# Experts' tokens loaded as squares of 32x32 and turned on VectorE, in a fused GNN, attention and mixture-of-experts kernel

## The chip, the cores and the metric

The kernel runs on one core of a Trainium2 chip. The metric is the device time of one execution in microseconds. A core has five engines with an instruction stream each: TensorE (PE, its weight loads are shown as PEld), VectorE (DVE), ScalarE (ACT), GpSimd (POOL) and SyncE (SP), which here only issues transfers. The transfers themselves run on 16 DMA engines.

## The reference, cut to what matters

One layer on 4096 tokens of 256 floats, all in fp32: an aggregation over a 4096x4096 adjacency matrix, causal attention with four heads, and then the part that the change touches, a mixture of 8 experts of which every token uses two.

```python
flat = _rmsnorm(x, ln2_w).reshape(-1, Cx)
probs = jax.nn.softmax(flat @ router_w.T, axis=-1)
tp, ti = jax.lax.top_k(probs, TOPK)
tp = tp / (jnp.sum(tp, axis=-1, keepdims=True) + 1e-09)
weights = jnp.sum(tp[..., None] * jax.nn.one_hot(ti, NE, dtype=flat.dtype), axis=1)
out = jnp.zeros_like(flat)
for e in range(NE):
    hh = jax.nn.silu(flat @ w1[e].T) * (flat @ w3[e].T)
    out = out + weights[:, e:e + 1] * (hh @ w2[e].T)
return x + out.reshape(Bx, Tx, Cx)
```

The hidden width is 682. The kernel computes an expert only for the tokens that chose it.

## The kernel before

Three stages follow each other: the aggregation to about 510 us, attention over eight blocks of 512 tokens to about 1027 us, the experts to the end. The stages overlap at their edges: the last attention block's normalization and output product run as "steps" between the products of the first expert groups.

**Lists.** As tokens are finished in attention they are written to a table `lists` in DRAM, sorted by expert. A row has 265 floats (`ROW` = 256 + 1 + 8): the token, its row number, and its 8 gates.

**Groups.** The experts' work is cut into groups of rows of one expert: 256 rows for the first 25 (`NW`), 128 for the rest; 42 are run (`NM`). `TURNS` is the order: nine large ones, then large and small mixed, mostly in turn (a "pair" below; at three places two small ones follow one large, a "double pair"), three large ones last. Loops run over k, a place in that order. `SEVEN` are the large groups from k = 4 to 39, whose second product is made of seven half-size products (Strassen's manner); `SPLIT13`, 13 of them (k from 12 to 39), do the same in the first product. Its sums of weights are made by GpSimd (`sums13`, L1463 to L1466), its sums of inputs by VectorE (`sums_x`, L1480).

**What a group needs.** `load13` (L1382, 1.4 MB) and `load2` (L1388, 0.77 MB) bring an expert's weights, `load_rows` (L1399) the group's rows, one transfer with a row on each partition. The expert and the first row come from a table, through registers. All three are issued by SP, each into one of five buffers in turn.

**Preparing a group.** `prepare(k)` turns the tokens so that features lie on partitions: TensorE transposes (L1413) into a PSUM tile `tx`, then ScalarE scales by the norm's weights into `xT` (L1419), `sums_x` where the group is in `SPLIT13`, and VectorE picks the expert's gate (`pick`, L1427, and a reduction, L1432). `hidden(k)` (L1698, L1704, L1705) or `hidden_seven(k)` (products L1525, ScalarE's copies of banks L1531, adds L1534, silu, multiplications L1563 and L1564) makes the first product and the gating, and calls `prepare` for the next group: after the first block of products where the next PSUM bank is free early (`early`, and before `SEVEN`), and otherwise at its end; `hidden_seven` does so after its third products. `combine(k-1)` (L1754, or L1655 with VectorE's adds L1663 to L1669) makes the second product, ScalarE or VectorE multiplies by the gate (L1765, L1771), and GpSimd adds the rows to DRAM at the row numbers (scatter, L1776).

**The loop.** Turn k: `hidden(k)` with `prepare(k+1)`, `combine(k-1)`, then GpSimd writes `sent` (L1910) and SP copies it to `sent_dram` (L1911), which makes SP wait until GpSimd has issued the scatters, then SP issues `load2(k+4)`, `load13(k+5)`, `load_rows(k+4)`; then GpSimd's `sums13`. Every engine executes in the order of its own queue. A framework puts in the semaphores; each DMA takes one of eight in rotation and waits for the one that had it before.

**The start of the experts.** `begin_experts` (L1789) issues the first loads late in attention (at 1018 us of the trace). `prepare(0)` is put two places before attention's end. The steps at the hand-over are: VectorE's totals of exponentials (L810), then for the last block the adding of two parts (L833), a reciprocal of the denominators (L845), a multiplication (L846), and then TensorE's output product po (L901).

Two lines tell much of the queues:

```python
nc.gpsimd.memset(sent, 0.0)
nc.sync.dma_start(sent_dram, sent)
```

Of the kernel before, what the change touches and what calls it, by code (L numbers as in the profile page):

```python
# [17 lines left out]
P = 128  # L18
N = 4096
C = 256  # L20
# [46 lines left out]
def fast_kernel(  # L67
# [618 lines left out]
    with (  # L686
# [14 lines left out]
        pt_all = sp.tile([P, 9 * 1024], F32, name="pt_all")  # L701
        late = sp.tile([P, 2 * (NF + 1) * GR + 4 * GR + 5 * 2 * ROW], F32, name="late")
        LATE_XT, LATE_ROWS = 2 * (NF + 1) * GR, 2 * (NF + 1) * GR + 4 * GR
        ring = [pt_all[:, n * 1024 : (n + 1) * 1024] for n in range(9)]
# [345 lines left out]
        def join(inst, group):  # L1050
            tc.add_to_no_dep_group(group, inst.ins)
# [320 lines left out]
        w2s = [a.rearrange("p (k c) -> p k c", k=NF + 1) for a in at2]  # L1372
        rows, hidden_of, inputs_of, expert_of, gates_of = {}, {}, {}, {}, {}

# [11 lines left out]
        def load2(k):  # L1386
# [4 lines left out]
            )  # L1391

        def load_rows(k):
            i = TURNS[k]
            n = halves(i)
            at = entry(table[0:1, 0, i : i + 1], NE * REG - (GR if i < NW else 0))
            r = late[:, LATE_ROWS + k % 5 * 2 * ROW : LATE_ROWS + (k % 5 + 1) * 2 * ROW]
            r = r.rearrange("p (h c) -> p h c", h=HALF)
            get = nc.sync.dma_start(  # L1399
                r[:, 0:n, :], lists[bass.ds(at, n * P), :].rearrange("(h p) c -> p h c", p=P)  # L1400
            )
            if i < NA:
                free(get, "late writes", "the rows of the first groups are whole by then")
                join(get, "first reads")
            rows[i] = r

        def prepare(k, pool=p_y, tag="y"):
            i = TURNS[k]
            n = halves(i)
            tr = pool.tile([P, 2, n, P], F32, tag=tag, name=f"tx_{i}")  # L1410
            for h in range(n):
                for c in range(2):
                    nc.tensor.transpose(  # L1413
                        tr[:, c, h, :], rows[i][:, h, c * P : (c + 1) * P], ident
                    )
# [11 lines left out]
            nc.vector.tensor_mul(  # L1427
                pick, rows[i][:, 0:n, C + 1 : ROW],
                mine[:, i : i + 1, :].to_broadcast([P, n, NE]),
            )  # L1430
            gates_of[i] = ex.tile([P, n, 1], F32, tag="gt", name=f"gt_{i}", bufs=3)
            nc.vector.tensor_reduce(gates_of[i], pick, AX.X, ALU.add)  # L1432
# [35 lines left out]

        def sums_x(k, tr):

# [6 lines left out]
            for dst, c, h, less in (  # L1477
                ("T1", 0, 1, "B11"), ("T2", 1, 1, "T1"), ("T3", 1, 1, "B12"), ("T4", 1, 0, "T2"),
            ):
                nc.vector.scalar_tensor_tensor(  # L1480
                    m[dst], tr[:, c, h, :], ln2_sb[:, c : c + 1], m[less],
                    op0=ALU.mult, op1=ALU.subtract,
# [3 lines left out]
        def hidden_seven(k, step, behind):  # L1486
# [99 lines left out]
            if behind is not None:  # L1586
                prepare(behind, p_ms, "ms")
            gated(two)
# [83 lines left out]
        def hidden(k, step=None, behind=None):  # L1672
# [3 lines left out]
            hT = hTs[k % 2][:, :, 0:n]  # L1676
            free_bank = k >= SEVEN[0]
            early = n == P and not (k - 1 in SEVEN and k - 2 in SEVEN)

            for q in range(0, NF + 1, 2):  # L1680
# [38 lines left out]
            )  # L1719
            if behind is not None and free_bank and not early:  # L1720
                prepare(behind, p_ms, "ms")
            hidden_of[i] = hT
# [3 lines left out]
        def combine(k):  # L1726
# [34 lines left out]
            for h in range(n):  # L1761
# [12 lines left out]
                at = bass.IndirectOffsetOnAxis(ap=r[:, h, C : C + 1].bitcast(I32), axis=0)  # L1774
                nc.gpsimd.memset(gap, 0.0)  # L1775
# [64 lines left out]
        for b in ORDER[:-1]:  # L1840
# [9 lines left out]
        later.setdefault(PLACES - 2, []).append(  # L1850
            lambda: [prepare(0, p_ms, "ms")] + [nc.gpsimd.memset(t[:, NF, :], 0.0) for t in hTs]
        )
# [36 lines left out]
        for k in range(NM):  # L1889
# [775 lines left out]
```

## Time and profile before

| | |
|---|---|
| time, median of three runs | 1532.2 us (1532.18 to 1532.7) |
| the profiled execution | 1532.31 us |
| its span in the trace | 1530.5 us |
| experts' stage | from about 1027 us to the end |
| a pair in that stage | 21.5 us |
| transposes of tokens on TensorE | 134 |

A profile is of one execution, and the span is the time from its first to its last instruction; 1.8 us lie around it. Times in the trace count from the span's start. A line of the timeline has start and length in us, the engine, the source line, the operation, what it writes and reads, shapes, and in brackets how long the engine stood idle before it and which instruction released it. Matmuls overlap each other in TensorE, so the length of one record (273 ns for a transpose) is more than what it costs in a row of them. The last 20 us hold scatters to the output that wait for a copy of the sums from DRAM to DRAM, issued at 1492.04 us in turn order (L1923).

### The profile page before, as it was taken

Reading aid. Unit: us, or ns where it says so; the run is one execution under the profiler, and the core shown is the slowest. Engines: PE = TensorE matmul, PEld = TensorE weight load, DVE = VectorE, ACT = ScalarE, POOL = GpSimd, SP = SyncE. Lnnn points to the kernel's source line nnn. Section 1 sums busy time; section 2 is a strip of 40 time slices with the busy share of each in tenths; the row PEclk is TensorE's granted clock in tenths of the full one; section 3 lists DMA queues with packets and bytes.
Section 4 is the critical chain, followed back from the end, with each engine's and each line's share of the span. In section 5 each row is a group of like instructions: output and inputs, shape, how many; then the busy total and the mean of one; then the engine's idle time right before and its main releaser. Section 6 shows DMA issues by size and latency. Waiting matters only on the chain. (4 is left out here: it accounts for less than half of the span.)

```text
span 1530.5 us, 28132 instructions
## 1 busy us (share of the span) xinstructions
PE 1518.1 (99%) x10925; PEld 1122.9 (73%) x10925; DVE 1056.4 (69%) x2182; ACT 555.6 (36%) x989; POOL 556.8 (36%) x641
## 2 busy tenths in 40 slices
PE   9999999999999999999999999999999999999997
PEld 8888888888888544444444444358899999999996
DVE  7764665755755677779879878785565777677762
ACT  2102012021021455655665655653122433343341
POOL 2102022121221331374554553442424445545342
PEclk9999999999999999999999999999999999999999
DMA  6334444543544000010011011048777787787845
GB/s 240 131 130 151 160 141 148 161 153 127 179 141 151 5 1 23 22 58 30 30 58 37 28 38 36 23 166 297 220 204 219 225 275 254 225 274 248 271 129 134
DMA packets 69595, 212.16 MB, mean 139 GB/s; under 512 B 17898, under 2 KB 45930, under 8 KB 55818
## 3 DMA queue, kind: packets, MB, share of 16 engines
q1 hardware_dynamic: 55914, 191.99, 36.4%
q0 software_dynamic: 12720, 17.47, 6.5%
q8 instruction: 88, 1.44, 0.4%
q10 hardware_dynamic: 816, 0.79, 0.2%
q14 instruction: 57, 0.47, 0.1%
HBM read 184.48 MB, written 27.13 MB: 138 GB/s over the span
## 5 line engine op out<-in xcount | busy, mean ns | idle before, releaser
L782 PE MATMUL sc<-qT_all,kT 64*64 64x512 f32 (+3 forms) x2304 | 282.1, 557 | 0.5 <-ACT pt_all L790 0.3
L532 PE MATMUL acc<-a,g 128*128 128x256 f32 x1024 | 244.0, 379 | 0.0
L532 PEld LDWEIGHTS acc<-a,g 128*128 128x128 f32 x1024 | 193.5, 190 | 31.8 <-issue 6.7
L782 PEld LDWEIGHTS sc<-qT_all,kT 64*64 64x64 f32 x2304 | 91.2, 133 | 128.6 <-issue 109.2
L790 ACT ACTIVATE pt_all<-sc 128x1024 f32<-128x1024 f32 (+3 forms) x157 | 148.8, 955 | 96.7 <-PE sc L782 94.6
L1776 POOL DMA_INDIRECT acc_dram<-y,late x40 | 62.8, 1571 | 178.0 <-ACT y L1765 118.5
L532 PE MATMUL acc<-more_sums,g 128*128 128x256 f32 x512 | 126.3, 379 | 0.0
L810 DVE TENSOR_TENSOR late<-late,pt_all 128x1024 f32<-128x1024 f32 (+3 forms) x91 | 107.5, 1181 | 24.3 <-POOL pt_all L792 9.8
L433 ACT COPY qT_all<-tr 128x512 f32<-128x512 f32 x30 | 16.2, 588 | 259.1 <-PE tr L431 259.1
L532 PEld LDWEIGHTS acc<-more_sums,g 128*128 128x128 f32 x512 | 97.2, 190 | 13.2
L824 PE MATMUL y_first<-pt_all,vv 64*64 64x512 f32 (+3 forms) x448 | 106.6, 554 | 0.0
L625 POOL TENSOR_TENSOR rot<-rot,tables 128x512 f32<-128x512 f32 x21 | 33.9, 1615 | 198.6 <-ACT rot L621 158.4
L1698 PE MATMUL h<-late,qT_all 128*128 128x256 f32 (+1 forms) x616 | 105.2, 327 | 0.0
L824 PE MATMUL y_second<-pt_all,vv 64*64 64x512 f32 (+3 forms) x436 | 104.2, 555 | 0.0
L1698 PEld LDWEIGHTS h<-late,qT_all 128*128 128x128 f32 x616 | 94.0, 191 | 9.6 <-ACT late L1419 0.8
L1060 POOL DMA_INDIRECT lists<-row,slots x64 | 87.4, 1366 | 17.1 <-issue 14.3
L1705 DVE TENSOR_TENSOR late<-si,h 128x256 f32<-128x256 f32 (+2 forms) x87 | 40.0, 467 | 73.7 <-ACT si L1704 42.7
L1704 ACT ACTIVATE si<-h 128x256 f32<-128x256 f32 (+2 forms) x87 | 36.5, 421 | 145.1 <-PE h L1698 142.2
L824 PE MATMUL y_third<-pt_all,vv 64*64 64x512 f32 (+3 forms) x372 | 88.7, 555 | 0.0
L621 ACT ACTIVATE rot<-pq 32x512 f32<-32x512 f32 x84 | 49.5, 589 | 82.6 <-DVE qT_all L619 43.6
L810 DVE TENSOR_TENSOR sum_all<-sum_all,pt_all 128x1024 f32<-128x1024 f32 (+3 forms) x51 | 56.0, 1097 | 15.5 <-POOL pt_all L792 9.2
L790 ACT ACTIVATE late<-sc 128x1024 f32<-128x1024 f32 (+3 forms) x55 | 50.9, 927 | 41.4 <-PE sc L782 38.4
(490 smaller groups left out, 3350.7 us busy)
## 6 DMA issues: line engine op xcount, KB each, us to landing
a<-in_adj_dram SPq DMA_DIRECT2D x64, 1024.0 KB
qT_all<-in_w_dram SPq DMA_DIRECT2D x18, 1408.0 KB
pt_all<-in_w_dram SPq DMA_DIRECT2D x16, 1408.0 KB
res_all<-in_w_dram SPq DMA_DIRECT2D x17, 768.0 KB
pt_all<-in_w_dram SPq DMA_DIRECT2D x16, 768.0 KB
res_all<-in_w_dram SPq DMA_DIRECT2D x8, 1408.0 KB
qT_all<-in_w_dram SPq DMA_DIRECT2D x9, 768.0 KB
late<-lists SPq DMA_DIRECT2D x25, 265.0 KB
```

The source lines that it names most:

```text
L532: nc.tensor.matmul(acc[bank][:, at, :], g[jb][:, right, k, :], m[left][:, k, :], start=(jb == 0 and k == 0 and at == 0), stop=(jb == NB - ...
L621: nc.scalar.activation(rot[n * Q : (n + 1) * Q, :], pj[(n ^ 1) * Q : ((n ^ 1) + 1) * Q, :], AF.Copy, scale=1.0 if n % 2 else -1.0,)
L625: nc.gpsimd.tensor_mul(rot, rot, tables[b][:, 1, :])
L782: nc.tensor.matmul(ps[k * HP : (k + 1) * HP, j, :w], kT[sb][hd, i * P + k * HP : i * P + (k + 1) * HP], qT[b][hd, p, off:], start=True, st ...
L790: nc.scalar.activation(pt[:, :, :w], ps[:, :, :w], AF.Exp, scale=HD ** -0.5)
L810: nc.vector.tensor_add(sums[b, p][:, :, off:], before[:, :, off:], pt[:, :, : 512 - off])
L824: nc.tensor.matmul(accs[b, p][k][hd, off:], vv[sb][some, i, hd], pt[some, j, : 512 - off], start=(s == order_of(b)[0]), stop=(s == order_o ...
L1060: put = nc.gpsimd.indirect_dma_start(out=lists[:, :], out_offset=bass.IndirectOffsetOnAxis(ap=chosen[b][:, k, t, :], axis=0), in_=flats[b] ...
L1698: nc.tensor.matmul(ps[m % 2][:, m // 2 - q, :], w13_sb[:, c, m * P : (m + 1) * P], xT[:, c, :], start=(c == 0), stop=(c == 1),)
L1704: nc.scalar.activation(si[:, 0:both, :], ps[0][:, 0:both, :], AF.Silu)
L1705: nc.vector.tensor_mul(hT[:, q : q + both, :], si[:, 0:both, :], ps[1][:, 0:both, :])
L1776: put = nc.gpsimd.indirect_dma_start(out=(acc_dram if k < NM - LAST else out)[:, :], out_offset=at, in_=y[:, h, :], in_offset=None, comput ...
```

## The change

Tokens are no longer loaded as rows. `load_squares(k)` issues eight transfers for a group: for each quarter of the partitions (32 of them) and each half of the features. A partition of the first transfer holds, of one token of each 32, the 32 features of one square; each piece read from DRAM is 32 floats, 128 bytes. Then one VectorE transpose, which turns every 32x32 square in place, gives features on partitions. It writes into the room that the squares of group k+4 use later (five rooms in turn), and ScalarE and `sums_x` read it from SBUF instead of PSUM. `load_rows` loads only the 9 last floats of each row. In `prepare` nothing is left for TensorE, and no PSUM bank is needed, so the two conditions on the bank go and `prepare(k+1)` always stands after the first block of `hidden(k)`. The column of the row number in the scatter becomes 0. `begin_experts` has a new order, with the first narrow rows behind w13(1).

```diff
+        KEPT = ROW - C
+        LATE_XT = 2 * (NF + 1) * GR
+        LATE_Z = LATE_XT + 4 * GR
+        LATE_ROWS = LATE_Z + 5 * 2 * C
+        late = sp.tile([P, LATE_ROWS + 5 * 2 * KEPT], F32, name="late")
...
+        def squares_room(k):
+            return late[:, LATE_Z + k % 5 * 2 * C : LATE_Z + (k % 5 + 1) * 2 * C]
+
+        def load_squares(k):
+
+            i = TURNS[k]
+            n = halves(i)
+            at = rows_at[i] = entry(
+                table[0:1, 0, i : i + 1], NE * REG - (GR if i < NW else 0)
+            )
+            z = squares_room(k)[:, 0 : n * C].rearrange("p (c m d) -> p c m d", c=2, d=Q)
+            tokens = lists[bass.ds(at, n * P), 0:C].rearrange(
+                "(m i) (c g d) -> g c i m d", i=Q, c=2, d=Q
+            )
+            for g in range(4):
+                for c in range(2):
+                    loaded(
+                        i, nc.sync.dma_start(z[g * Q : (g + 1) * Q, c], tokens[g, c])
+                    )
...
-            get = nc.sync.dma_start(
-                r[:, 0:n, :], lists[bass.ds(at, n * P), :].rearrange("(h p) c -> p h c", p=P)
-            )
+            loaded(i, nc.sync.dma_start(
+                r[:, 0:n, :],
+                lists[bass.ds(rows_at.pop(i), n * P), C:].rearrange("(h p) c -> p h c", p=P),
+            ))
...
-        def prepare(k, pool=p_y, tag="y"):
+        def prepare(k):
             i = TURNS[k]
             n = halves(i)
-            tr = pool.tile([P, 2, n, P], F32, tag=tag, name=f"tx_{i}")
-            for h in range(n):
-                for c in range(2):
-                    nc.tensor.transpose(
-                        tr[:, c, h, :], rows[i][:, h, c * P : (c + 1) * P], ident
-                    )
+            turned = squares_room(k + 4)[:, 0 : n * C]
+            nc.vector.transpose(turned, squares_room(k)[:, 0 : n * C])
+            turned = turned.rearrange("p (c i) -> p c i", c=2)
             xT = late[:, LATE_XT + k % 2 * 2 * GR : LATE_XT + k % 2 * 2 * GR + 2 * n * P]
             xT = xT.rearrange("p (c i) -> p c i", c=2)
             for c in range(2):
                 nc.scalar.activation(
-                    xT[:, c, :], tr[:, c].rearrange("p h i -> p (h i)"), AF.Copy,
-                    scale=ln2_sb[:, c : c + 1],
+                    xT[:, c, :], turned[:, c, :], AF.Copy, scale=ln2_sb[:, c : c + 1]
                 )
             inputs_of[i] = xT
             if k in SPLIT13:
-                sums_x(k, tr)
+                sums_x(k, turned)
             pick = ex.tile([P, n, NE], F32, tag="pick", name=f"pick_{i}")
             nc.vector.tensor_mul(
-                pick, rows[i][:, 0:n, C + 1 : ROW],
+                pick, rows[i][:, 0:n, 1:KEPT],
                 mine[:, i : i + 1, :].to_broadcast([P, n, NE]),
             )
...
                 if q == 0 and behind is not None:
-                    if not free_bank:
-                        prepare(behind)
-                    elif early:
-                        prepare(behind, p_ms, "ms")
+                    prepare(behind)
...
-            if behind is not None and free_bank and not early:
-                prepare(behind, p_ms, "ms")
...
         def begin_experts():
             make_table(NB - 1, True, 0, NA)
-            load_rows(0)
+            load_squares(0)
             load13(0)
-            load_rows(1)
+            load_squares(1)
             load2(0)
             load13(1)
-            load_rows(2)
+            for k in range(2):
+                load_rows(k)
+            load_squares(2)
             load2(1)
-            load_rows(3)
+            load_squares(3)
+            for k in range(2, 4):
+                load_rows(k)
...
             if k + 4 < NM:
+                load_squares(k + 4)
                 load_rows(k + 4)
```

More of the change, by code (lines that the diff above doesn't have):

```diff
@@ L701, in fast_kernel @@
         pt_all = sp.tile([P, 9 * 1024], F32, name="pt_all")
-        late = sp.tile([P, 2 * (NF + 1) * GR + 4 * GR + 5 * 2 * ROW], F32, name="late")
-        LATE_XT, LATE_ROWS = 2 * (NF + 1) * GR, 2 * (NF + 1) * GR + 4 * GR
+        KEPT = ROW - C
[3 more added lines that the diff above has]
+        late = sp.tile([P, LATE_ROWS + 5 * 2 * KEPT], F32, name="late")
         ring = [pt_all[:, n * 1024 : (n + 1) * 1024] for n in range(9)]
@@ L1372, in fast_kernel @@
         w2s = [a.rearrange("p (k c) -> p k c", k=NF + 1) for a in at2]
-        rows, hidden_of, inputs_of, expert_of, gates_of = {}, {}, {}, {}, {}
+        rows, hidden_of, inputs_of, expert_of, gates_of, rows_at = {}, {}, {}, {}, {}, {}
         def halves(i):
@@ L1391, in load2, with loaded @@
             )
+        def loaded(i, get):
+            if i < NA:
+                free(get, "late writes", "the rows of the first groups are whole by then")
+                join(get, "first reads")
+        def squares_room(k):
[15 more added lines that the diff above has]
+                    )
         def load_rows(k):
@@ L1395, in load_rows @@
             n = halves(i)
-            at = entry(table[0:1, 0, i : i + 1], NE * REG - (GR if i < NW else 0))
-            r = late[:, LATE_ROWS + k % 5 * 2 * ROW : LATE_ROWS + (k % 5 + 1) * 2 * ROW]
+            r = late[:, LATE_ROWS + k % 5 * 2 * KEPT : LATE_ROWS + (k % 5 + 1) * 2 * KEPT]
             r = r.rearrange("p (h c) -> p h c", h=HALF)
-            get = nc.sync.dma_start(
-                r[:, 0:n, :], lists[bass.ds(at, n * P), :].rearrange("(h p) c -> p h c", p=P)
-            )
-            if i < NA:
-                free(get, "late writes", "the rows of the first groups are whole by then")
-                join(get, "first reads")
+            loaded(i, nc.sync.dma_start(
+                r[:, 0:n, :],
+                lists[bass.ds(rows_at.pop(i), n * P), C:].rearrange("(h p) c -> p h c", p=P),
+            ))
             rows[i] = r
-        def prepare(k, pool=p_y, tag="y"):
+        def prepare(k):
             i = TURNS[k]
             n = halves(i)
-            tr = pool.tile([P, 2, n, P], F32, tag=tag, name=f"tx_{i}")
-            for h in range(n):
-                for c in range(2):
-                    nc.tensor.transpose(
-                        tr[:, c, h, :], rows[i][:, h, c * P : (c + 1) * P], ident
-                    )
+            turned = squares_room(k + 4)[:, 0 : n * C]
+            nc.vector.transpose(turned, squares_room(k)[:, 0 : n * C])
+            turned = turned.rearrange("p (c i) -> p c i", c=2)
             xT = late[:, LATE_XT + k % 2 * 2 * GR : LATE_XT + k % 2 * 2 * GR + 2 * n * P]
@@ L1467, in sums13, with sums_x @@
             sums13_of[k] = m
-        def sums_x(k, tr):
+        def sums_x(k, turned):
             xT = inputs_of[TURNS[k]]
@@ L1480, in sums_x @@
                 nc.vector.scalar_tensor_tensor(
-                    m[dst], tr[:, c, h, :], ln2_sb[:, c : c + 1], m[less],
+                    m[dst], turned[:, c, h * P : (h + 1) * P], ln2_sb[:, c : c + 1], m[less],
                     op0=ALU.mult, op1=ALU.subtract,
@@ L1676, in hidden @@
             hT = hTs[k % 2][:, :, 0:n]
-            free_bank = k >= SEVEN[0]
-            early = n == P and not (k - 1 in SEVEN and k - 2 in SEVEN)
             for q in range(0, NF + 1, 2):
@@ L1708, in hidden @@
                 if q == 0 and behind is not None:
-                    if not free_bank:
-                        prepare(behind)
-                    elif early:
-                        prepare(behind, p_ms, "ms")
+                    prepare(behind)
                 if step and q < NF - 1:
@@ L1719, in hidden @@
             )
-            if behind is not None and free_bank and not early:
-                prepare(behind, p_ms, "ms")
             hidden_of[i] = hT
@@ L1773, in combine @@
                     )
-                at = bass.IndirectOffsetOnAxis(ap=r[:, h, C : C + 1].bitcast(I32), axis=0)
+                at = bass.IndirectOffsetOnAxis(ap=r[:, h, 0:1].bitcast(I32), axis=0)
                 nc.gpsimd.memset(gap, 0.0)
@@ L1850, in fast_kernel @@
         later.setdefault(PLACES - 2, []).append(
-            lambda: [prepare(0, p_ms, "ms")] + [nc.gpsimd.memset(t[:, NF, :], 0.0) for t in hTs]
+            lambda: [prepare(0)] + [nc.gpsimd.memset(t[:, NF, :], 0.0) for t in hTs]
         )
```

## The prediction

> **What bounds the kernel now.** I read the busy shares first, then the waits of TensorE in the expert stage, then that stage by lines, then one pair of groups in order of time, last the hand-over from attention to the experts.
>
> The page's busy shares, the DMA share over 40 slices, and the expert stage by lines (busy us, mean ns | idle before):
>
> ```profile
> PE 1518.1 (99%) x10925; PEld 1122.9 (73%) x10925; DVE 1056.4 (69%) x2182; ACT 555.6 (36%) x989; POOL 556.8 (36%) x641
> ...
> DMA  6334444543544000010011011048777787787845
> ...
> L1413 PE MATMUL tx<-ident,late 128*128 128x128 f32 x134 | 21.6, 273 | 0.0
> L1413 PEld LDWEIGHTS tx<-ident,late 128*128 128x128 f32 x134 | 16.3, 142 | 1.9 <-issue 0.8
> ```
>
> TensorE is the bound; the view of its waits is empty from 1040 to the tail. The 134 transposes (L1413) are pipelined: four take 0.44 us between weight loads (1185.55 to 1185.99), so 0.115 us each and 15.4 us in all. That is the most the change can take off TensorE. But the DMA is 70 to 80% busy in this stage, and VectorE is not far off:
>
> ```profile
> 1272.93 1.56 POOL L1464 TENSOR_TENSOR sum_all<-sum_all,qT_all 128x640 f32<-128x640 f32 x1
> 1274.43 0.16 DVE L1427 TENSOR_TENSOR pick<-late,mine 128x8 f32<-128x8 f32 x1
> 1274.57 1.54 POOL L1465 TENSOR_TENSOR sum_all<-qT_all,sum_all 128x640 f32<-128x640 f32 x1
> 1274.70 1.95 DVE L1563 TENSOR_TENSOR late<-qT_all,hy 128x512 f32<-128x512 f32 x1
> ...
> 1281.26 0.42 DVE L1705 TENSOR_TENSOR late<-si,h 128x256 f32<-128x256 f32 x1
> 1281.59 0.34 DVE L1480 SCALAR_TENSOR_TENSOR kT<-tx,ln_sb,late 128x128 f32<-128x128 f32 x1
> ...
> 1287.95 0.29 DVE L1666 TENSOR_TENSOR vv<-vv,ye_ms 128x128 f32<-128x128 f32 x1 [0.57 <-PE ye_ms L1655]
> 1289.53 0.57 ACT L1531 COPY wqkv_sb<-hA 128x512 f32<-128x512 f32 x1
> 1290.42 1.06 PE L1525 MATMUL hA<-kT,sum_all 128*128 128x128 f32 x8
> ```
>
> This is the timeline of one pair (a 256-row group of seven products and a 128-row one), which recurs every 21.5 us (`sent` at 1186.45, 1207.97, 1229.51). In a pair VectorE waits for TensorE only at L1666, 0.57 us: that is all the slack of its loop. And ScalarE's copy of hA ends 1290.10, 0.32 us before TensorE reuses the bank. L1563 ends 0.54 us after GpSimd's L1465 (1276.65 against 1276.11); away from GpSimd it takes 0.68.
>
> The hand-over, VectorE and TensorE:
>
> ```profile
> 1029.66 0.17 DVE L1427 TENSOR_TENSOR pick<-late,mine 128x16 f32<-128x16 f32 x1
> 1029.95 0.68 DVE L833 TENSOR_TENSOR yT<-yT,y_second 128x512 f32<-128x512 f32 x1
> ...
> 1033.38 3.35 DVE L845 RECIPROCAL rden<-rden 128x512 f32<-128x512 f32 x1 [0.49 <-ACT rden L844]
> 1036.77 0.69 DVE L846 TENSOR_TENSOR yT<-yT,rden 128x512 f32<-128x512 f32 x1
> ...
> 1027.53 3.72 PE L1698 MATMUL h<-late,qT_all 128*128 128x256 f32 x16
> ...
> 1038.77 1.05 PE L901 MATMUL po<-wo_sb,yT 128*128 128x264 f32 x4
> ```
>
> The last attention block's normalization (L833 to L846) and the first groups share VectorE; TensorE takes po (L901) 1.3 us after L846 ends.
>
> **What the Trainium skill says.** "VectorE: DVE Perf Modes", "The three transpose paths": VectorE turns only 32x32 blocks, which is why the transfer must place the squares. "SBUF — State Buffer", "Who interferes with whom": an elementwise VectorE operation with two SBUF inputs and GpSimd's SBUF work shut each other out for a whole instruction; one with at most one SBUF input does not contend. The trace agrees: L1563 0.68 alone, 1.95 beside L1465; transposes (L311) run beside GpSimd's L165 and L166 at their usual length. sums_x (L1480) now has two SBUF inputs, but GpSimd is idle there (1280.3 to 1289.4): 0. "DMA: Bandwidth & Descriptors", "Specifications": pieces under 512 B miss the line rate. Squares come in pieces of 128 B.
>
> **The change, part by part.**
>
> *TensorE:* −134 transposes, −15.4 us if nothing else binds.
>
> *VectorE:* +42 transposes. The nearest rows are the 32x512 ones:
>
> ```profile
> L311 DVE STREAM_TRANSPOSE tables<-tables x14: 659/680/704, 111.1 to 470.0; 32x512 f32<-32x512 f32 x14
> ```
>
> I take 0.65 us for 128x512 and 0.33 for 128x256, as the length per partition decides. Bounds: at least a plain pass (0.42 and 0.2 by L1705), at most four times if quadrants were served one by one (2.7), which no other VectorE row suggests.
>
> One turn of the VectorE loop in a pair, A = start of L1666: y (ScalarE, A+0.64), GpSimd's scatters and then L1463 to L1465, ended at A+9.69; L1563 freed at A+10.23; L1705, sums_x, picks, the adds; L1666 again possible at A+20.97, while TensorE gives it at A+21.53. The 256-row transpose now stands in that loop, after the first L1705, and all behind it (sums_x, pick, the other L1705, the adds) moves: +0.65. sums_x then waits for ScalarE's xT, which itself waits for the transpose: two hand-overs of 0.05 and one 0.42 activation, +0.5. (Before, that ran in the shade of L1705.) The 128-row transpose stands ahead of L1563, which waits for GpSimd anyway: 0. So 20.97+0.65+0.5 = 22.1 against 21.5: +0.55 for each of 9 pairs, +5.0, and TensorE's 0.115x6 = 0.7 a pair is not realised. Three double pairs (two 128-row groups to one) get half as much more room: +1.2 by the same count.
>
> A collision is possible: with the 128-row transpose in front, pick (two SBUF inputs) would start at A+8.2, and L1465 starts at A+8.15. Where pick is caught, it and L1563 wait for a GpSimd operation more, 1.57 us. Bounds 0 and 9x1.57 = 14; half of it, +7, as the two times agree within 0.1 us.
>
> Groups 2 to 12 have no GpSimd sums and VectorE has room: there TensorE keeps what it saves, 8x0.46+0.23 = 3.9 and 0.7. Groups 40 and 41: −0.9.
>
> *ScalarE* reads SBUF instead of PSUM: 0.416 (L1557) against 0.472 (L1419), within its idle time: 0.
>
> *DMA:* a 256-row group takes 2048 pieces of 128 B. The rate from three windows of the aggregation (us, PE, PEld, DVE, ACT, POOL busy, clock, DMA share, GB/s):
>
> ```profile
> 449.00:453.00 4.00, 4.00 (x21) 3.51 (x20) 3.86 (x5) 0.37 (x1) 1.95 (x2) 1.00 0.72 262
> 455.00:460.00 5.00, 5.00 (x25) 4.41 (x24) 3.54 (x7) 0.00 (x0) 0.00 (x0) 1.00 0.79 238
> 461.00:465.00 4.00, 4.00 (x20) 3.51 (x19) 2.59 (x11) 0.00 (x0) 0.00 (x0) 1.00 0.75 262
> ...
> 1261.00:1492.00 231.00, 231.00 (x1879) 225.61 (x1878) 166.73 (x387) 89.06 (x221) 112.84 (x120) 1.00 0.77 234
> ```
>
> The middle one holds 1024 such pieces besides the same 1 MB: 5x0.79 = 3.95 against 2.9 us of all engines, so 1.02 us for 1024. A pair's squares take 3.1 us, the narrow remainder some 0.4, and old rows of 1.1 us go: about +2.4 us on 0.77–0.81 of 21.5 = 17 us. 19.4 of 22 fits. At twice the packet cost, 22.5 of 22: it would bind. Nothing hides it then.
>
> *SP:* per group 8 transfers and 8 register loads more. Narrow transfers of the denominators (L863) took 2.44 us for four, their register work included, so +4.9 us a turn. Its turn begins when `sent_dram` has waited for GpSimd, at `sent` w13 is issued about 1.6 us later and lands after 8.2–8.6; the semaphores of DMAs go round by eight, so a group's last square waits for that w13. With 0.6 for it and 0.6 for rows: 10.1 us, against 10.75 for an average turn. It fits by 0.6, and loads have two turns of lead; cost 0, at most what the DMA rival has.
>
> *Hand-over:* squares(0) is issued from 1017.97 to 1022.2 (eight at about 0.6), its transpose takes pick's old place at 1029.66 behind the totals; xT and the first hidden product come at 1030.9 instead of 1027.53. Squares of group 1 end with the wait for w13(0), landed about 1028.9; then w2(0), w13(1), and only then rows(0), issued at about 1031.1 behind 2.2 MB: landed about 1038 (2.2 MB at 360 GB/s, the rate of a 1 MB load alone, are 6.1 us). pick(0) stands on VectorE right behind the transpose and waits for it; behind it are queued L833, L1705, transpose(1), pick(1), L845, L846. L846 then ends at about 1044.6 instead of 1037.5, po about 1044.7 instead of 1038.77: +5.9, the first two groups' transposes included. If rows(0) came by 1031, only the 3.4 us late start would remain, and some of that is made up: the low bound is +2; rows 3 us later still is +9.
>
> Sum: 5.9 −3.9 −0.7 +5.0 +7.0 +1.2 −0.9 = +13.6, against the profiled execution of 1532.31 (span 1530.5 and 1.8 around it), 0.1 above the median of 1532.2. So 1546.
>
> **Rivals.**
> 1. *VectorE has more room than I count* (the other side). Place: the pair's loop; if sums_x's wait for xT is covered, or the tile's order lets L1563 start earlier, its slack exceeds 1.2 us, TensorE stays the bound and the saving comes through. 1532.3−15.4+5.9 = 1523; with the hand-over made up, 1517. It decides from a pair of under 21.5 us. For: VectorE is only 69% busy. Against: 0.57 us of slack at L1666. Chance 0.18.
> 2. *Both cancel*, pairs at 21.4–21.6 us with the stall at the start: 1529–1535. Chance 0.10.
> 3. *The transfers bind*: packets cost 30 ns or more (16 measured), or SP's turn passes 10.75 us through the wait for w13, and weights come late. +1 to 2 us a turn in some 30 turns: 1555–1600, mid 1572. For: DMA share 0.8 already and both margins under 10%. Against: two turns of lead. Chance 0.17.
>
> **How the numbers follow.** Main case (VectorE's loop and the stall) 1535–1558, chance 0.55. Low 1522 holds nearly all of rival 1, high 1572 half of rival 3. A measurement here tells 0.2%, 3 us, from no change. Faster 0.18, same 0.10, slower 0.55+0.17 = 0.72.
>
> **What would show it.** Right: the pair lengthens to 22–23.5 us, L1666's wait for TensorE vanishes, TensorE shows waits for VectorE or ScalarE at the hidden products of seven; pick(0) waits for its transfer at about 1030 to 1038; po starts near 1045; DMA share 0.85–0.9. Wrong: TensorE still without waits and pairs of 20.8 (rival 1); TensorE waiting for w13 or VectorE's transposes for squares in steady groups (rival 3); transposes well off 0.65 us.

## The result, and the profile after

The changed kernel takes 1568.1 us (median of four runs, 1563.1 to 1571.2) against 1532.2 before: a ratio of 1.023, with an interval of 1.020 to 1.026. It is 36 us slower; 14 were forecast. The runs of the changed kernel lie 8 us apart, those of the kernel before 0.6.

The page of the kernel after, busy shares and the rows of 40 slices:

```profile
PE 1521.0 (97%) x10791; PEld 1121.4 (72%) x10791; DVE 1073.7 (69%) x2224; ACT 554.3 (35%) x989; POOL 554.9 (35%) x641
...
PEclk9999999999999999999999999989999999999999
DMA  6443444444443000011011011079878887777765
```

TensorE fell from 99% to 97% of a longer span although 134 of its instructions are gone. The DMA row is about as it was; one slice of the stage, from about 1057 us, reaches nine tenths. The waits tell where to look. First TensorE's in the expert stage (line waited for: us in total, times, longest), then VectorE's, then those of SyncE's queue from 1180 to 1500:

```profile
PE hA L1546 <- issue: 19.8, 10, 5.0
PE po L904 <- DVE yT L849: 3.4, 1, 3.4
...
DVE late L1436 <- DMA late<-lists: 18.7, 7, 4.6
...
SPq L1418 <- DMA qT_all<-in_w_dram: 33.3, 11, 4.7
SPq L1418 <- DMA pt_all<-in_w_dram: 32.9, 12, 4.0
SPq L1418 <- DMA res_all<-in_w_dram: 15.3, 5, 4.7
```

TensorE had no wait at all there before. Now the second product of hA in a group of seven stands for up to 5 us. VectorE's transposes (L1436) waited seven times for squares. And SyncE, which issues squares at L1418, waits 81 us in this stretch for the landing of expert weights (w2 or w13). For the same stretch of the kernel before, the same view has at its top only waits for GpSimd, which is SyncE with nothing to do:

```profile
SPq L1911 <- POOL sent L1910: 111.7, 12, 9.7
SPq L1911 <- POOL gap L1775: 92.1, 16, 6.2
```

In the changed kernel SyncE waits for GpSimd for 0.7 us in all of this stretch: it is always behind.

One turn of SyncE after, in order of time (start, length in us; a length over several transfers includes the waits between them):

```profile
1232.18 0.28 SPq L1928 DMA_DIRECT2D sent_dram<-sent  x1
1232.72 0.37 SPq L1391 DMA_DIRECT2D res_all<-in_w_dram  x1
1233.79 0.35 SPq L1385 DMA_DIRECT2D pt_all<-in_w_dram  x1
1234.72 8.63 SPq L1418 DMA_DIRECT2D late<-lists  x8
1243.62 0.52 SPq L1426 DMA_DIRECT2D late<-lists  x1
1244.24 0.30 SPq L1928 DMA_DIRECT2D sent_dram<-sent  x1
```

12.06 us from one `sent` to the next, 8.63 of them in the eight squares. The forecast had 10.1. A turn of the kernel before, with w2 (left out), w13 and the rows:

```profile
1186.45 0.29 SPq L1911 DMA_DIRECT2D sent_dram<-sent  x1
...
1188.03 0.33 SPq L1382 DMA_DIRECT2D qT_all<-in_w_dram  x1
1188.99 0.38 SPq L1399 DMA_DIRECT2D late<-lists  x1
1199.00 0.29 SPq L1911 DMA_DIRECT2D sent_dram<-sent  x1
```

There SyncE was done 2.9 us after `sent` and then waited for the next one.

How a late square becomes a wait at hA, in the timelines of VectorE, ScalarE and TensorE:

```profile
1455.21 0.71 DVE L1436 STREAM_TRANSPOSE late<-late 128x512 f32<-128x512 f32 x1 [4.61 <-DMA late<-lists]
...
1462.86 1.03 ACT L1778 ACTIVATE y<-vv,gt 128x256 f32<-128x256 f32 x2 [4.98 <-DVE vv L1688]
1463.80 0.57 ACT L1552 COPY wqkv_sb<-hA 128x512 f32<-128x512 f32 x1
...
1464.46 2.05 PE L1546 MATMUL hA<-kT,sum_all 128*128 128x128 f32 x8 [5.00 <-issue]
```

The transpose waits 4.61 us; all of VectorE's work behind it, up to the adds of the second product, is that much later; ScalarE's y waits for those adds, and its copy of the bank hA stands behind y; TensorE needs the bank.

To see where the time goes, I take from each trace the start of each group's second product and subtract that of the kernel before (us; k is the turn):

```
k                  0     10     13     20     26     34     41
after            10.7    6.8    9.5   13.3   15.2   31.5   35.5
```

So 10.7 us are lost ahead of group 0's second product, 4 come back up to turn 10, and 29 are lost from turn 11 on, in a few jumps.

TensorE's own account of the 35.5: it waits 33 us in the stage; while its clock is halved (last section) it works for 25.7 us, of which half, 13 us, is lost; and the transposes that are gone give back 15.4 by the forecast's estimate. That makes 30; the other 5 are not located.

### The profile page after: what moved, and what is told of

The parts are those of the page before. It is cut to its first block, busy times and chain, and to the rows that moved or that the text cites. A ratio compares the mean times of both kernels' runs of the same rounds, so it can differ in the third digit from the quotient of the medians.

```text
span 1566.0 us, 29265 instructions
## 1 busy us (share of the span) xinstructions
PE 1521.0 (97%) x10791; PEld 1121.4 (72%) x10791; DVE 1073.7 (69%) x2224; ACT 554.3 (35%) x989; POOL 554.9 (35%) x641
## 5 line engine op out<-in xcount | busy, mean ns | idle before, releaser
L793 ACT ACTIVATE pt_all<-sc 128x1024 f32<-128x1024 f32 (+3 forms) x157 | 148.8, 955 | 96.7 <-PE sc L785 95.2
L1441 ACT ACTIVATE late<-late,ln_sb 128x256 f32<-128x256 f32 (+1 forms) x84 | 34.5, 457 | 115.5 <-DVE late L1436 102.4
```

Source lines behind the costliest of these rows:

```text
L793: nc.scalar.activation(pt[:, :, :w], ps[:, :, :w], AF.Exp, scale=HD ** -0.5)
L1441: nc.scalar.activation(xT[:, c, :], turned[:, c, :], AF.Copy, scale=ln2_sb[:, c : c + 1])
```

## The experiments

Three theories stood against each other: Q, SyncE's queue; V, VectorE's loop; P, the DMA engines' time for small pieces. Each edit below is against the changed kernel unless another is named. Where it says "another arrangement", the numbers multiplied are the tokens' own but differently placed.

**One transfer a group** (leaves VectorE's part of the change alone)

```diff
-            for g in range(4):
-                for c in range(2):
-                    loaded(i, nc.sync.dma_start(z[g * Q : (g + 1) * Q, c], tokens[g, c]))
+            r = squares_room(k)[:, 0 : n * C].rearrange("p (h c) -> p h c", c=C)
+            loaded(i, nc.sync.dma_start(
+                r, lists[bass.ds(at, n * P), 0:C].rearrange("(h p) c -> p h c", p=P)))
```

> The changed kernel, but a group's tokens come in one transfer of whole rows (1 KB pieces) instead of eight of squares; VectorE still turns 32x32 blocks, so what is multiplied are the tokens' floats in another arrangement. It leaves the VectorE part of the change alone. Three theories of where the 36 us come from: Q, SyncE's queue: a turn of it takes 11.5 to 12 us because the last squares wait for the w13 just issued; V, VectorE's loop with the transposes; P, the DMA engines' time for small pieces. Q and P expect 1520 to 1535 here; V expects 1555 or more; the recorded sum's VectorE terms alone would give 1537 to 1545.

Measured: 1545.2 us (1544.8 to 1545.4), ratio 1.008 (1.0065 to 1.0099). Without the squares' loads the change costs 13 us, start included. The whole recorded sum was 13.6, and the range expected here for its VectorE terms ended at 1545. The other 23 come with the loads.

**The loads alone** (TensorE turns, VectorE doesn't)

```diff
-            nc.vector.transpose(turned, squares_room(k)[:, 0 : n * C])
+            for h in range(n):
+                for c in range(2):
+                    nc.tensor.transpose(tr[:, c, h, :],
+                        squares_room(k)[:, (c * n + h) * P : (c * n + h + 1) * P], ident)
```

> The changed kernel's loads as they are (squares, narrow rows, their order), but turned by TensorE into PSUM at the places where the kernel before did it, so that VectorE has nothing to turn; what is multiplied are the tokens' floats in another arrangement. It leaves the loads alone. Q and P expect 1560 to 1580 (no saving on TensorE, the same late loads); V expects 1535 to 1543, which is the stall at the start only.

Measured: 1573.4 us (1572.3 to 1577.6). The loads alone cost 41, so V alone is out. Together the two parts cost less than their sum, 36 against 54. That one engine catches up while another stalls would explain it, but is not shown.

**Weights behind the squares**

```diff
+                load_squares(k + 4)
+                load_rows(k + 4)
                 load2(k + 4)
             if k + 5 < NM:
                 load13(k + 5)
-            if k + 4 < NM:
-                load_squares(k + 4)
-                load_rows(k + 4)
```

> The changed kernel with one edit: in a turn the squares and narrow rows are issued before w2 and w13, so that the last squares wait for the w13 of the turn before. The same transfers and bytes. Q expects that SyncE's turn falls under 10.7 us and the time to 1530 to 1548; P and V expect 1563 to 1571, as before the edit.

Measured: 1569.8 us (1565.3 to 1572.3): nothing gained, against Q as I had put it. The trace says why this does not settle it. GpSimd now waited for w13 before its sums, L1484, up to 10 us at a time:

```profile
1342.80 1.54 POOL L1484 TENSOR_TENSOR sum_all<-qT_all 128x640 f32<-128x640 f32 x1 [10.08 <-DMA qT_all<-in_w_dram]
1424.29 1.53 POOL L1484 TENSOR_TENSOR res_all<-pt_all 128x640 f32<-128x640 f32 x1 [10.32 <-DMA pt_all<-in_w_dram]
```

and SyncE still waited 50 us for weights from 1180 to 1500, beside 35 us for GpSimd. A mean turn took 11.6 us, as in the changed kernel: one late thing was traded for another.

**Narrow rows early**

```diff
             load_squares(0)
+            load_rows(0)
             load13(0)
             load_squares(1)
+            load_rows(1)
             load2(0)
             load13(1)
-            for k in range(2):
-                load_rows(k)
```

> The changed kernel with one edit at the start: the narrow rows of groups 0 and 1 are issued right behind their squares and ahead of the weights. The stall of VectorE at the first pick (10.4 us) goes, and TensorE starts group 0 at about 1031 all the same. If nothing behind absorbs it: 6 to 8 us less, 1560 to 1562. If Q holds and SyncE's turn alone sets the pace from group 12 on, part of it is eaten: 1562 to 1568.

Measured: 1560.9 us (1557.6 to 1564.7), 7 less. In the traces it is 6.2 us behind the kernel before at turn 0, instead of 10.7, and 30.1 at the end, instead of 35.5.

**Eight transfers of larger pieces**

```diff
-            z = squares_room(k)[:, 0 : n * C].rearrange("p (c m d) -> p c m d", c=2, d=Q)
-                "(m i) (c g d) -> g c i m d", i=Q, c=2, d=Q
+            z = squares_room(k)[:, 0 : n * C].rearrange("p (c m d) -> p c m d", c=2, d=P)
+                "(m g i) (c d) -> g c i m d", g=4, i=Q, c=2, d=P
```

> The changed kernel with its eight transfers a group, in the same order and with the same waits, but each moves pieces of 512 B (32 partitions, half a row each) in place of 128 B: a quarter of the pieces. What is multiplied are the tokens' floats in another arrangement. After one_transfer (1545) and squares_pe (1573) the loads are known to cost; this parts number from size. Q (number of transfers, and the wait for w13 among them) expects 1560 to 1572, P (small pieces keep the DMA engines busy) expects 1545 to 1553.

Measured: 1563.9 us (1561.4 to 1567.0). A quarter of the pieces and nearly all of the loss: P explains some 4 us at the most, and the runs of the two kernels overlap.

**Squares on both sides of the weights**

```diff
+                load_squares(k + 4, (0, 1))
                 load2(k + 4)
             if k + 5 < NM:
                 load13(k + 5)
             if k + 4 < NM:
-                load_squares(k + 4)
+                load_squares(k + 4, (2, 3))
                 load_rows(k + 4)
```

> The changed kernel with four of a group's squares issued ahead of w2 and w13 and four behind them, so that no square waits for a weight of its own turn, and w13 is only 2.5 us later than in the changed kernel (in weights_last it was 6 to 8 us later, and GpSimd's sums waited for it up to 10 us). Q with the in-turn wait as its heart expects 1548 to 1556; P expects 1563 to 1571.

Measured: 1567.5 us (1564.8 to 1569.9); a miss for Q in this form. SyncE still waited 62 us for weights from 1180 to 1500 (by the order of issue now for that of the turn before), a mean turn took 11.7 us, and GpSimd waited 34 us for w13. By the count, with twelve transfers a turn and eight semaphores, a wait for a transfer of 1.4 MB falls somewhere in every turn, whatever the order. A form without it has to have at most eight.

**Four transfers a group, 256 B pieces**

```diff
-            z = squares_room(k)[:, 0 : n * C].rearrange("p (c m d) -> p c m d", c=2, d=Q)
+            z = squares_room(k)[:, 0 : n * C].rearrange("p (m e) -> p m e", e=2 * Q)
...
-                "(m i) (c g d) -> g c i m d", i=Q, c=2, d=Q
+                "(m i) (g e) -> g i m e", i=Q, g=4
...
-                for c in range(2):
-                    loaded(i, nc.sync.dma_start(z[g * Q : (g + 1) * Q, c], tokens[g, c]))
+                loaded(i, nc.sync.dma_start(z[g * Q : (g + 1) * Q], tokens[g]))
...
+    w13_q = w13.reshape(NE, W13, 4, 2, Q).transpose(0, 2, 4, 3, 1).reshape(NE, P, 2, W13)
```

(The norm's weights are dealt out in the same way, and ScalarE and sums_x read the turned room with a stride.)

> Features are dealt to partitions so that a quarter of the partitions takes 64 neighbouring floats of a token: four transfers a group of 256 B pieces, half of both. Eight transfers make a turn, so each waits for its own kind of the turn before. Rows of w13 and the norm's weights are permuted to match. If the loads' cost is gone: 1547 to 1553 (VectorE's 12 us and a start of about +6 remain). If P holds and the time goes with the pieces: about 1556.

Measured: 1546.1 us (1544.9 to 1547.2), the time of one transfer. The DMA engines are busier than in the changed kernel (share 0.87 against 0.79 from 1180 to 1480), and yet SyncE waits only 7 us for weights where it waited 81. It is back to waiting for GpSimd (its queue, 1180 to 1500):

```profile
SPq L1927 <- POOL sent L1926: 82.7, 12, 8.7
SPq L1927 <- POOL gap L1787: 45.7, 16, 4.8
SPq L1385 <- DMA pt_all<-in_w_q_dram: 4.4, 6, 1.3
```

**Four transfers and four single floats** (against four_transfers)

```diff
                 loaded(i, nc.sync.dma_start(z[g * Q : (g + 1) * Q], tokens[g]))
+                if k >= 4:
+                    nc.sync.dma_start(small_dram[:, g : g + 1], ident[0:1, 0:1])
```

> four_transfers (1546) with four transfers of a single float added to each group's loads from the fifth turn on, one behind each square: twelve transfers a turn again, as in the changed kernel, at the bytes and piece sizes of four_transfers. If the number of transfers, with the waits that it brings, is what the changed loads cost (Q): 1558 to 1570, and SyncE's turns 11 to 12.5 us instead of 8 and 12 to 14 in turn. If it is bytes or pieces: 1545 to 1548.

Measured: 1560.3 us (1558.2 to 1568.1). Four transfers of 4 bytes a turn bring back 14 of the 22 us between four_transfers and the changed kernel, and the waits of SyncE. The other 8 are not explained by this run; by eight_large, up to 4 of them may be the smaller pieces. w13 is an input of its own here (in_w_q), so they are plainly waits for w13 (SyncE's queue, 1180 to 1500):

```profile
SPq L1418 <- DMA pt_all<-in_w_q_dram: 52.8, 12, 5.6
SPq L1418 <- DMA qT_all<-in_w_q_dram: 49.7, 10, 6.1
SPq L1418 <- DMA res_all<-in_w_q_dram: 19.6, 5, 4.7
```

**Half of each w13** (the other half of the product uses an older group's weights)

```diff
+            if k < 7:
...
+            else:
+                nc.sync.dma_start(w13s[k % 5][:, 0],
+                    w13[bass.ds(expert_of[i], 1), :, 0].rearrange("o p w -> (o p) w"))
```

> The changed kernel with only half of each w13 loaded from the eighth group on (what is multiplied there in the other half is an older group's weights), so that each w13 lands some 3 us sooner. If the landing of w13, waited for inside SyncE's turn, makes the turn long: turns of 9 to 10 us and 1545 to 1553. If the issuing of twelve transfers itself does: turns stay at 11 to 12 us and the time at 1560 or more.

Measured: 1550.6 us (1549.3 to 1555.3). The same twelve transfers, but from 1180 to 1500 eight squares took 4.4 to 7.4 us where they took 6.3 to 9.5, and SyncE waits for GpSimd again (41 us, beside 39 for weights). So it is not the issuing alone but the landing of w13, waited for inside the turn. This edit also takes bytes off the DMA engines. That bytes alone are not the cause is shown by four_transfers and four_and_small, which move the same bytes (but for 16 a turn) and differ by 14 us.

Mean of SyncE's last 27 turns, from the starts of the `sent` transfers in each trace:

```
                 mean us   shortest   turns under 9.5 us   time
before             10.4       8.2           15             1532.2
after              11.6       9.6            0             1568.1
eight_large        11.7      10.3            0             1563.9
four_and_small     11.9      10.2            0             1560.3
half_w13           10.9       8.7            6             1550.6
four_transfers     10.8       8.1           12             1546.1
one_transfer       10.9       8.1           10             1545.2
weights_last       11.6       7.3            6             1569.8
squares_split      11.7       7.8            5             1567.5
```

The turns are those of the profiled execution, which was the slowest one for four_and_small (1568.1) and half_w13 (1555.3); the times are medians. The mean is the pace of the whole loop, whoever sets it; the short turns tell more. A turn that follows TensorE is short for a small group and long for a large one. Where no turn is under 9.5 us, SyncE sets the pace. In the two kernels of another order SyncE waits for GpSimd at some turns, and GpSimd for w13 at others.

**VectorE's loop taken apart.** The next kernels are built on four_transfers with rows_early. In a group of seven, the next transposes stand where VectorE waits for TensorE, and the next pick behind the multiplications:

```diff
             sums2(k)
+            turn(k + 1)
+            turn(k + 2)
             begun(one)
...
             if behind is not None:
-                prepare(behind)
+                prepare(behind, False)
...
             multiplied(two)
+            if behind is not None:
+                pick_gates(behind)
```

> four_transfers with three more edits: narrow rows of groups 0 and 1 ahead of the weights; in a group of seven products the transposes of the next two groups stand at its start, where VectorE waits for TensorE; and the pick of the next group stands behind the multiplications, out of GpSimd's way. If V's terms are right, VectorE's loop in a pair falls from 22.1 to about 21 us and the 12 us go too: 1522 to 1532. If they are not, 1541 to 1546.

Measured: 1548.7 us (1544.2 to 1550.8), a miss: slower than either branch. Most pairs now take 20.9 us (before: 21.5), so the instructions moved here are what had made pairs longer; but at three places, where two small groups had gone before, the squares had not landed, and 4.4 to 5.6 us went each time.

**Squares first**: the order of weights_last on top, and `turn(k + 2)` behind the first additions.

> four_turned_ahead (1548.6), which already has pairs of 20.9 us but lost 4 to 5 us at three places where VectorE waited for the squares of the group after next, with two edits: squares and narrow rows are issued ahead of w2 and w13, and the second transpose stands behind the first additions. If those waits were all: 1529 to 1535, faster than one_transfer by 10 or more. If VectorE's loop is the bound in another way: 1540 or more.

Measured: 1534.7 us (1529.8 to 1545.2), ratio 1.0012 (0.9998 to 1.0026). Better by 14, but GpSimd waited 5 us at a time for w13 again.

**Group 0 earlier**: the whole of `prepare(0)` three places earlier.

> The same with the first group's transpose three places earlier, ahead of the last totals of attention, so that TensorE need not stand for 4.1 us before group 0. If the squares have landed by then: 3 to 5 us less than four_squares_first; if not, or if the delayed totals cost as much: within 1 us of it, or slower.

Measured: 1539.1 us (1537.0 to 1543.4), a miss. ScalarE's scaling of group 0 stood in its queue 7.3 us for the transpose, ahead of attention's exponentials (L793), and TensorE waited 6.1 us for those.

**Second transpose later, weights first**

> four_turned_ahead (1548.6) with the weights ahead of the squares as there, but the transpose for the group after next stands behind the first additions, some 3 us later in VectorE's queue. If the waits for squares (three places, 4 to 5 us each) were the only thing left: 1524 to 1530, faster than the kernel before. If the transposes so placed are themselves in VectorE's way: 1533 to 1540.

Measured: 1538.9 us (1537.3 to 1542.8), not the hoped-for range. Most pairs take 20.9 us, and the same three places are left.

**Order w13, squares, rows, w2**

> The same with the order in a turn w13, squares, narrow rows, w2: squares land some 2 us sooner, and w13 is not put off as in four_squares_first, where GpSimd's sums waited for it 5 us at a time; w2 is 4 us later. 1523 to 1529, at or under four_second_later; if w2 then comes late for VectorE's sums of it, 1532 or more.

Measured: 1536.6 us (1536.3 to 1537.8). A miss that pays: no wait for squares is left, and still TensorE stands 2.2 us at the three places. VectorE there, sums_x in its four instructions (L1514), beside GpSimd's sums:

```profile
1241.19 3.02 DVE L1514 SCALAR_TENSOR_TENSOR kT<-late,ln_sb 128x128 f32<-128x128 f32 x1 [0.57 <-ACT late L1447]
1244.24 1.57 DVE L1514 SCALAR_TENSOR_TENSOR kT<-late,ln_sb,kT 128x128 f32<-128x128 f32 x1
1245.74 1.69 DVE L1514 SCALAR_TENSOR_TENSOR kT<-late,ln_sb 128x128 f32<-128x128 f32 x1
1247.35 1.62 DVE L1514 SCALAR_TENSOR_TENSOR kT<-late,ln_sb,kT 128x128 f32<-128x128 f32 x1
...
1241.90 2.15 POOL L1497 TENSOR_TENSOR res_all<-pt_all 128x640 f32<-128x640 f32 x1
1244.13 1.54 POOL L1498 TENSOR_TENSOR res_all<-res_all,pt_all 128x640 f32<-128x640 f32 x1
```

7.9 us where it takes 1.4 elsewhere. Each instruction of VectorE ends just behind one of GpSimd's: 1244.21 against 1244.05, 1245.81 against 1245.67. one_transfer has the same 7.9 us at the same three places.

**At those places, turn into PSUM**

```diff
             turned = squares_room(k + 4)[:, 0 : n * C]
+            if into_psum:
+                turned = p_ms.tile([P, n * C], F32, tag="ms", name=f"tz_{k}")
```

> four_w13_first (1536.6) with one edit: where a large group follows two small ones, its transpose writes to a bank of PSUM instead of SBUF, so that sums_x reads one operand from PSUM again. There sums_x took 7.9 us for four instructions instead of 1.4, beside GpSimd's sums, and TensorE then stood for 2.2 us, three times. If those two SBUF operands are the third limit: the three stalls go and 1527 to 1531 is left. If it is the place and not the operands: 1535 to 1538.

Measured: 1527.9 us (1527.0 to 1528.5), ratio 0.997 (0.9957 to 0.9981). The three places are quick again (VectorE at the first of them, and GpSimd's sum beside it):

```profile
1242.58 0.35 DVE L1516 SCALAR_TENSOR_TENSOR kT<-tz,ln_sb,late 128x128 f32<-128x128 f32 x1 [0.91 <-ACT late L1449]
1242.96 0.35 DVE L1516 SCALAR_TENSOR_TENSOR kT<-tz,ln_sb,kT 128x128 f32<-128x128 f32 x1
1243.23 0.34 DVE L1516 SCALAR_TENSOR_TENSOR kT<-tz,ln_sb,late 128x128 f32<-128x128 f32 x1
1243.49 0.34 DVE L1516 SCALAR_TENSOR_TENSOR kT<-tz,ln_sb,kT 128x128 f32<-128x128 f32 x1
...
1242.95 2.14 POOL L1499 TENSOR_TENSOR res_all<-pt_all 128x640 f32<-128x640 f32 x1
```

Three of the four run inside GpSimd's sum and keep their length. So the second SBUF operand was the cause, and not the place.

**Only the transpose of group 0 earlier**

```diff
+        later.setdefault(PLACES - 5, []).append(lambda: turn(0))
```

> The same with the transpose of group 0 alone three places earlier, ahead of the last totals, and ScalarE's scaling of it left where it was (in four_squares_first_start it was moved too and held up the exponentials for 7 us). If TensorE's 4.1 us before group 0 hang on that transpose: 3 to 6 us less than four_psum_doubles, 1522 to 1527. If not: the same within 1 us.

Measured: 1525.3 us (1523.5 to 1527.9), ratio 0.995 (0.9937 to 0.9964): 7 us faster than the kernel before. The further gain, 2.7 us, falls just short of the forecast. It can't be placed: the profiled execution was the slowest of the five (1527.9), and its trace is 0.9 us ahead of four_psum_doubles at turn 0 and 0.3 at the end. TensorE still stands 3.1 us ahead of group 0, now for w13(0).

## Why the prediction was wrong

The direction was right and the size was not: +14 forecast, +36 measured. By its own steps:

**The step that failed: SyncE.** "10.1 us, against 10.75 for an average turn. It fits by 0.6 ... cost 0." A turn took 11.6 us in the mean. The mis-sized term is the landing of w13, for which the last square waits. The sum put it at 8.2 to 8.6 us. By the DMA packets in the trace of the kernel before, the last packet of w13 ended 7.8 us after the issue of w13 (median of 30 turns, 6.8 to 9.0), and 9.5 us after `sent` (8.4 to 10.6). So 8.2 to 8.6 fits a count from the issue, and a sum of 10.1 has no room for the 1.6 us from `sent` to the issue (1186.45 and 1188.03 above). With them it is 11.7 by my estimate, over the 10.75. In the changed kernel the last square was issued 10.3 us after `sent` (mean of 30 turns), and the next `sent` came 1.3 us later; in the turn shown above the squares ended at 1243.35, 11.2 us after `sent`. The two turns of lead only put the cost off: the first transpose that waited for squares came at 1268.7 us, waits of 1.1 to 4.6 us from 1349.7 on. From turn 11 on the difference between the changed kernel and one_transfer grows by 16.5 us (6.3 at turns 0 and 10, 22.8 at the end). I had the mechanism as a rival, with its place and the value it decides from, but as an alternative to the main case. It came on top.

The Trainium skill bears on it: "DMA: Bandwidth & Descriptors", "Anatomy of one DMA — SWDGE (gpsimd) path", says, in a section on GpSimd's transfers, that the DMA engines do not wait on semaphores, and that any such wait is held on the issuing sequencer ahead of the dispatch. The trace of SyncE agrees: a wait for one transfer holds all that are behind it in the issuing queue, as the 8.63 us above show.

**The start, mis-sized.** +5.9 forecast, 10.7 measured at turn 0. The mechanism is the one described. VectorE's pick and its wait, the reciprocal's product, and TensorE's two waits:

```profile
1040.81 0.17 DVE L1448 TENSOR_TENSOR pick<-late,mine 128x16 f32<-128x16 f32 x1 [10.42 <-DMA late<-lists]
1047.84 0.69 DVE L849 TENSOR_TENSOR yT<-yT,rden 128x512 f32<-128x512 f32 x1
...
1030.98 6.17 PE L1716 MATMUL h<-late,qT_all 128*128 128x256 f32 x16 [4.11 <-ACT late L1441]
1048.58 0.71 PE L904 MATMUL po<-wo_sb,yT 128*128 128x264 f32 x2 [3.40 <-DVE yT L849]
```

pick(0) was put at 1038.0 and came at 1040.8; L849 ends at 1048.5, not 1044.6. And the first product took 6.17 us where it took 3.72: a term that the sum lacked, the halved clock (last section). rows_early shows that the rows' place in the order is worth 7 us of the whole, 4.5 of them at turn 0.

**VectorE's loop, right in sum and in part by luck.** From turn 10 to the end one_transfer loses 12.3 us. The sum's terms for these turns (−0.7, 5.0, 7.0, 1.2, −0.9) give 11.6. But its pairs do not take 22.1 us each: by the starts of second products, of the ten pairs with a single small group three take 20.9, two 21.8 to 21.9, three 23.0 to 23.1 and two 24.6 to 24.7. And VectorE waited for TensorE not only at L1666, as the forecast read it: in the kernel before, L1534 waits too, 1.62 us at 1290.69, which is room that four_turned_ahead uses. The collision that I took at half did come: in the changed kernel,

```profile
1210.32 1.49 DVE L1448 TENSOR_TENSOR pick<-late,mine 128x8 f32<-128x8 f32 x1
1211.92 1.91 DVE L1584 TENSOR_TENSOR late<-wqkv_sb,hy 128x512 f32<-128x512 f32 x1
...
1226.21 1.03 ACT L1778 ACTIVATE wo_sb<-vv,gt 128x256 f32<-128x256 f32 x2 [5.14 <-DVE vv L1688]
1227.14 0.57 ACT L1552 COPY qT_all<-hA 128x512 f32<-128x512 f32 x1
...
1227.81 1.13 PE L1546 MATMUL hA<-kT,res_all 128*128 128x128 f32 x8 [2.35 <-issue]
```

pick is caught behind GpSimd (L1486, to 1211.79), L1584 behind the next of its operations (L1487, to 1213.28), VectorE's adds are late, ScalarE's y is late, the copy of hA stands behind it in ScalarE's queue, and TensorE waits 2.35 us for the bank (the view says "issue", since it found no semaphore to blame). The forecast's 0.55 and 1.57 make 2.12. What was wrong inside this sum is "GpSimd is idle there: 0" for sums_x. That holds for the pairs whose timeline I had read and not for the three double pairs, where it costs 6.5 us of VectorE each time once the second operand is in SBUF (four_w13_first and four_psum_doubles; the same 7.9 us stand in one_transfer). In the changed kernel itself sums_x has its 1.4 us everywhere, as other waits had shifted it: there this cost lay hidden. In one_transfer it is part of the 12.3, against a term of nothing.

**TensorE's saving, right.** Turns 0 to 10 gain 3.95 us (forecast for groups 2 to 10: 3.9). With all three limits out of the way (four_psum_doubles), the pairs but the first take 20.9 us.

**The transfers, right for the engines.** At 16 ns a piece the DMA engines were said to have room, and eight_large shows that the pieces cost some 4 us at the most. The DMA share of 0.85 to 0.9 that was to show the main case right did not come in the changed kernel (0.77 to 0.83), where the same bytes had more time; it is 0.87 in four_transfers.

**Rivals 1 and 2** did not come, and the measured time lies in the range of rival 3, at a chance of 0.17. The changed kernel has stretches without a stall (turns 14 to 17, 22 to 25), but the jumps between them ate what they gained. Rival 1's way to a gain is real, though, with the edits of four_psum_doubles.

## What to carry to other kernels

Before splitting one transfer into eight, count the transfers of a turn against the semaphores that they rotate through and write out what each one waits for: beyond one rotation a turn, a small transfer waits for a large one of the same turn or of the one just before, and all behind it in the queue waits too. Count every term of such a sum from the same moment. Two limits that each have a thin margin are not alternatives; add them. Whoever moves an operand from PSUM to SBUF should look at every place where that VectorE instruction runs, and not only at the one that recurs most.

## What the runs showed of the hardware that was not expected

A wait of TensorE is paid more than once. In these windows of the changed kernel, at the ends of waits of 2.14 and 5.00 us, the granted clock is near half (us, busy PE, PEld, DVE, ACT, POOL, clock, DMA share, GB/s):

```profile
1302.00:1306.00 4.00, 3.68 (x19) 3.71 (x20) 0.69 (x1) 1.30 (x3) 3.81 (x5) 0.57 0.58 177
1462.00:1468.00 6.00, 3.54 (x16) 3.57 (x17) 1.86 (x6) 2.56 (x5) 2.23 (x3) 0.55 0.40 73
```

Eight matmuls that take 1.06 us took 2.05 in both places. Over the run the mean clock fell from 0.999 to 0.989. Of that, TensorE's work felt some 13 us: before its last product there are six stretches of half clock, of 3.4 or 6.8 us, and it works for 25.7 us of them. That was in no term of the sum. How much of the 36 us it makes is not shown, since part of it falls where SyncE sets the pace.

"TensorE: Matmul & The Clock Gate", "What's actually happening", of the Trainium skill states the mechanism, a halved clock after an idle window of about 3.4 us. Here less was enough, and the traces show what decides. In all 18 the stretches of half clock begin at whole multiples of 3.41 us from one another, so the clock goes by a fixed raster. Among raster stretches at full clock, all 82 in which TensorE stood idle for 0.55 of the time or more (1.9 us) were followed by half clock, and of those with less than 0.54 none. So the place of a wait in the raster counts beside its length: the wait of 2.14 us before 1302.32 lies in one stretch, which is 0.59 idle. The wait of 2.35 us before 1227.81 is cut by a border, into stretches with 0.49 and 0.20, and the products after it took 1.13 us.

A forecast of a stall of 2 us or more should carry a term for the clock: one stretch of full work at half clock loses 1.7 us. That this makes the wider scatter of the runs with stalls (8 us, against 1.5 us for four_psum_doubles) is argued, not shown.
